# Fetching the turned rows on GpSimd's queue, and emitting row statistics and adjacency sums further behind their loads

## The chip, the cores and the metric

The kernel runs on one core of a Trainium2 chip. The core has five engines, each with an instruction queue that it works off in order: PE (TensorE, matrix products), DVE (VectorE), ACT (ScalarE), POOL (GpSimd) and SP (SyncE, which in this kernel only starts DMA transfers). An engine waits at an instruction until the semaphores of everything that it depends on have come. The metric is the device time of one execution in microseconds; lower is better.

## The reference

Two graph layers work on `x` of shape 128 x 128 x 256 (graphs, nodes, features) with an adjacency `adj` of 128 x 128 x 128. Cut to what matters:

```python
h = relu(layernorm(x))                       # layer 0
conv = relu(conv17(relu(conv1(h))) + h)      # along the nodes, with folded norms
msg  = relu(h @ w_msg + b_msg)
nmp  = (exp(-dist(h)) * adj) @ msg
x = x + gru(concat(conv, nmp), h)            # three gates

h = relu(layernorm(x))                       # layer 1, nodes 0..24 alone
for g, idx in enumerate(GROUPS):             # five groups of 25, 9, 7, 6, 6 nodes
    A = normalised(adj[:, idx][:, :, idx] + I)
    out = relu(A @ relu(A @ h[:, idx] @ W1[g] + b1[g]) @ W2[g] + b2[g])
    fused[:, idx] += softmax(fusion_w)[g] * out
x = x + fused
```

Layer 1 changes only the first 25 nodes of a graph. The other rows of the result are those of layer 0.

## The kernel before

Graphs are worked in 32 groups of four (`q`). The first 650 us or so do the convolution in frequency space, in two halves of 16 groups, and the messages of the groups that are ready. Then the last stage runs everything else together: `stage_c(q)` computes the gates of one group (matrix products of line 742; where no layer-1 work comes between, one group follows the next by some 33 us), and layer 1 follows in eight blocks of four groups.

The order in which instructions are emitted is set by a planner written into the kernel. Each piece of work is a generator, and each `yield cost, wait` says how much PE time the step just emitted is worth, and after how many further units of planned time its next step may be emitted. Lanes of generators are served by weight. The planner runs when the kernel is built; on the chip every engine simply takes its instructions in that order. A larger wait at a `yield` thus places the following instructions further back in their engines' queues; it makes nobody wait by itself.

The path of one group's result, with the lines that the change and the steps of the prediction touch:

- `stage_c` ends with the last gate sums on DVE (L854 to L867). PE's last product of the group goes into a bank that DVE must have read first (L862). POOL then runs six operations (L872 to L874, "the gates"), DVE turns the result (L897, emitted in the next group's `stage_c`) and adds the input rows (L904).
- `returned` stores the turned rows `xt` to DRAM (`x1d`) with four DMAs on POOL's queue (L906). The next group's input rows are loaded into the same buffer `xt` by POOL (L822).
- `fetch(q)` (L911 to L924) waits in the plan until `returned` has been emitted, then issues on SP's queue: L921 loads the first 32 nodes of the four graphs, 128 KB, into `X1`; L922 copies the other nodes, 384 KB, from `x1d` to the output, DRAM to DRAM. Both depend on the four stores.
- `rows(q)` (L963 to L980) computes mean and variance of the fetched rows on DVE (L971 to L973), the power -1/2 on POOL (L974), and the normalised rows `x1h` on DVE and ACT (L977, L978). They feed PE's L1058.
- `prepare(blk)` (L982 to L1044) loads the 25 x 25 adjacency of 16 graphs on SP (L990), adds the identity on POOL (L996, eight operations), sums rows on DVE (L1001), and makes the normalised adjacency with small PE products (L1007, L1012, L1033, L1038) and DVE and POOL operations between them; L1042 copies it to where L1058 reads it.
- `block(blk)` runs layer 1 for the block: L1058, then for each of the five groups two products (L1075, L1084). The weights `w1` are loaded on SP (L961) into two buffers, each load behind the last use of its buffer. At the end L1106, L1118 and L1128 turn, gather and fuse, and L1133 stores the rows on POOL's queue.
- SP's queue also holds the loads of `hTc` (L682), `xm` (L684) and `yt` (L606) for the next group.

Of the kernel before, what the change touches and what calls it, by code (L numbers as in the profile page):

```python
# [20 lines left out]
GB = 4  # L21
NQ = B // GB
# [9 lines left out]
QS = SB // GB  # L32
# [9 lines left out]
WIDE = 32  # L42


def _runs():

    out = []
    for g, nodes in enumerate(GROUPS):
        i = 0
        while i < len(nodes):  # L50
            j = i
            while j + 1 < len(nodes) and nodes[j + 1] == nodes[j] + 1:
                j += 1
            out.append((OFFS[g] + i, nodes[i], j - i + 1))
            i = j + 1
    return out
# [151 lines left out]
def kernel(ctx: ExitStack, tc: tile.TileContext, x, adj, consts, vecs, w_se, conv1_w,  # L208
                    conv2_w, w_msg, b_msg, w_ih, w_hh, W1, W2, b2, fusion_w, out):
    nc = tc.nc  # L210
# [15 lines left out]
    x1d = [dr.tile([GB, N, D], FP, name=f"x1d{q}") for q in range(NQ)]  # L226
# [7 lines left out]
    def c(name):  # L234
        a, b = CAT[name]
        return cst[:, a:b]
# [333 lines left out]
    EN, IN, IN2, X1, E_DONE, F_DONE = {}, {}, {}, {}, set(), set()  # L570
# [340 lines left out]
    def fetch(q):  # L911

        while q not in T_DONE:
            yield 0.0, 0.5
        yield 0.0, 12.0 if q < NQ - 1 else 6.0
        blk = q // QS
        while blk > 2 and blk - 3 not in F_DONE:
            yield 0.0, 0.5
        if blk not in X1:
            X1[blk] = LATE["co"].tile([P, QS, D], FP, tag="x1", name=f"x1_{blk}", bufs=3)  # L920
        nc.sync.dma_start(out=X1[blk][:, q % QS], in_=x1d[q][:, :WIDE])  # L921
        nc.sync.dma_start(out=out[q * GB:(q + 1) * GB, WIDE:], in_=x1d[q][:, WIDE:])  # L922
        yield 0.0, 5.0
        C_DONE.add(q)  # L924


# [55 lines left out]
    def prepare(blk):  # L982

        while not (blk - 1 in P_DONE and blk - 2 in {-2, *B1_DONE}):
            yield 0.0, 1.0
        pool, pool2, b1 = S["pool"], S["pool2"], S["b1"]
        ac, r4 = S["ac"][blk % 2], S["r4"][blk % 2]
        aj = pool.tile([NN, SB, NN], FP, tag="dd", name=f"aj{blk}")
        for i in range(GB):
            nc.sync.dma_start(out=aj[:, i % 2 * 2 + i // 2::GB],  # L990
                              in_=adj[blk * SB + i:(blk + 1) * SB:GB, :NN, :NN]
                              .rearrange("b n m -> n b m"))
        yield 0.0, 4.0

        for r, n, w in _runs():
            nc.gpsimd.tensor_tensor(b1[:, :, r:r + w], aj[:, :, n:n + w],  # L996
                                    ident[:NN, None, n:n + w].to_broadcast([NN, SB, w]),
                                    ALU.add)
        dg = pool2.tile([NN, SB, NG], FP, tag="dg", name=f"dg{blk}")
        for g in range(NG):  # L1000
            nc.vector.reduce_sum(dg[:, :, g], b1[:, :, OFFS[g]:OFFS[g] + SIZES[g]],  # L1001
                                 axis=mybir.AxisListType.X)
        yield 0.0, 7.0

        pa = ptmp.tile([P, SB // 2, RP], FP, tag="tmp", name=f"pa{blk}")
        for p in range(SB // 2):
            nc.tensor.matmul(pa[:, p], b1[:, 2 * p:2 * p + 2, :].rearrange("n s r -> n (s r)"),  # L1007
                             c("et")[:NN, :RP], start=True, stop=True)
        nc.vector.tensor_mul(ac, pa, c("same")[:, None, :].to_broadcast([P, SB // 2, RP]))

        pdg = ptmp.tile([P, SB // 2, 2, NG], FP, tag="tmp", name=f"pdg{blk}")
        nc.tensor.matmul(pdg.rearrange("p a s g -> p (a s g)"), c("et")[:NN],  # L1012
                         dg.rearrange("n b g -> n (b g)"), start=True, stop=True)
        dsel = pool.tile([P, SB // 2, 2 * NG], FP, tag="dsel", name=f"dsel{blk}")
        nc.vector.tensor_mul(dsel, pdg.rearrange("p a s g -> p a (s g)"),
                             c("sgrp")[:, None, :].to_broadcast([P, SB // 2, 2 * NG]))
        dm = pool.tile([P, SB // 2], FP, tag="dm", name=f"dm{blk}")
        zo = pool.tile([P, SB // 2], FP, tag="zo", name=f"zo{blk}")
        nc.vector.reduce_sum(dm, dsel, axis=mybir.AxisListType.X)
        nc.vector.tensor_scalar(zo, dm, 0.0, None, op0=ALU.is_equal)  # L1020
        nc.vector.tensor_add(dm, zo, dm)
        nc.gpsimd.tensor_tensor(dm, dm, c("mhalf"), ALU.pow)
        nc.gpsimd.tensor_mul(zo, zo, dm)
        nc.gpsimd.tensor_sub(dm, dm, zo)
        yield 2.0, 7.0

        dd = pool.tile([P, SB // 2, RP], FP, tag="dd", name=f"dd{blk}")
        nc.vector.tensor_mul(dd, c("diag")[:, None, :].to_broadcast([P, SB // 2, RP]),
                             dm[:, :, None].to_broadcast([P, SB // 2, RP]))
        nc.vector.tensor_mul(ac, ac, dm[:, :, None].to_broadcast([P, SB // 2, RP]))  # L1030
        yield 0.0, 6.0
        pg = ptmp.tile([P, SB // 2, RP], FP, tag="tmp", name=f"pg{blk}")
        nc.tensor.matmul(pg, c("ones2"), dd, start=True, stop=True)  # L1033
        nc.vector.tensor_mul(ac, ac, pg)
        yield 0.9, 3.0

        pr4 = ptmp.tile([P, QS, 2, RP], FP, tag="tmp", name=f"pr4{blk}")
        nc.tensor.matmul(pr4.rearrange("p q a r -> p (q a) r"), c("e4"), ac,  # L1038
                         start=True, stop=True)
        for j in range(GB):  # L1040
            s = slice(j * WIDE, (j + 1) * WIDE)
            nc.vector.tensor_copy(r4[s, :, j % 2 * 2 + j // 2, :], pr4[s, :, j % 2, :NR])  # L1042
        yield 0.9, 1.0
        P_DONE.add(blk)  # L1044
# [112 lines left out]
    for bat, (during_a, during_b) in enumerate(((0.66, 0.5), (0.2, 0.65))):  # L1157
        if bat:
# [12 lines left out]
    loads = Lane([stage_n(q) for q in range(NQ)])  # L1171
    groups = Lane([stage_c(q) for q in range(NQ)], ahead=2)
    second = [setup_1()] + [part(blk) for blk in range(NBLK) for part in (prepare, block)]
    beside.weight = 0.5
    order.run(loads, groups, beside, Lane([fetch(q) for q in range(NQ)], ahead=2),
              Lane([rows(q) for q in range(NQ)], ahead=2),
              Lane(second, ahead=2, weight=0.2))
# [41 lines left out]
```

## Time and profile before

| | us |
|---|---|
| median of three runs | 2040.95 |
| lowest and highest | 2039.93, 2042.65 |
| the profiled execution, its own time | 2045.82 |
| span of that execution, first to last instruction | 2043.9 |
| PE busy in it | 1975.7 |
| POOL busy in it | 865.4 |

The profile shows one execution. For every group of instructions it has the busy time and what ended the engine's idle time before it; a chain of waits follows the instruction that ended last back to what released it; busy time can be had for any stretch of the span, and every wait by the instruction that ended it. Names such as `x1d<-xt` say which tile is written and which is read.

### The profile page before, as it was taken

The page shows a single profiled execution, that of the slowest core. Times are in us where ns is not written, and L with a number is a line of the kernel's source. Part 1 is how long each engine was busy: PE and PEld are TensorE (multiplying, and loading weights), DVE is VectorE, ACT ScalarE, POOL GpSimd, SP SyncE. Part 2 cuts the span into 40 slices and gives each one's busy share as a digit, 9 for nine tenths or more (in the row PEclk, how much of TensorE's full clock was granted, in tenths as well). Part 3 has the DMA queues.
Part 4 walks back from the last instruction along what each step waited for, and adds up shares of the span by engine and source line. Part 5 has one row for each costly group of instructions (what it writes and reads, how often), then busy time and mean ns, then how long its engine had stood idle before and what let it go on. Part 6 is the DMA issues. An engine that isn't in the chain of part 4 may idle for free.

```text
span 2043.9 us, 33427 instructions
## 1 busy us (share of the span) xinstructions
PE 1975.7 (97%) x12596; PEld 1635.6 (80%) x12596; DVE 1327.4 (65%) x2807; ACT 683.3 (33%) x1547; POOL 865.4 (42%) x1026
## 2 busy tenths in 40 slices
PE   7998999999999999999889999999999999999988
PEld 5667888888888888878678878888788788888865
DVE  6774445875433667856774786778677868786542
ACT  4653222444222344222223232232323332322233
POOL 3542666333665133633441445335434444353330
PEclk9999999999999999999989999999999999999989
DMA  9987879654777644624423353343443533442331
GB/s 215 293 276 224 275 252 288 203 166 155 268 257 247 179 117 117 166 73 109 107 75 96 94 117 90 105 121 94 118 109 87 116 110 95 114 102 77 81 85 53
DMA packets 182583, 302.84 MB, mean 148 GB/s; under 512 B 24001, under 2 KB 131462, under 8 KB 182166
## 3 DMA queue, kind: packets, MB, share of 16 engines
q1 hardware_dynamic: 143238, 185.46, 31.6%
q0 software_dynamic: 38800, 114.96, 20.4%
q8 instruction: 100, 1.64, 0.3%
q14 instruction: 61, 0.50, 0.1%
q10 hardware_dynamic: 384, 0.28, 0.0%
HBM read 204.12 MB, written 109.05 MB: 153 GB/s over the span
## 4 chain that ended last, share of the span: by engine, by line
PE 83%; DVE 5%; DMA 5%; POOL 3%; issue 2%; SPq 1%; ACT 1%; DVEq 0%; POOLq 0%; ACTq 0%
PE p L742 38%; PE pa L527 7%; PE ph L1075 5%; PE pm L631 5%; PE pz L1084 5%; PE pc L422 4%; PE pb L527 3%; PE pf L433 3%; PE pi L699 3%; PE px L657 3%; PE pw L475 1%; PE ph L411 1%; PE py L1058 1%; DMA x1d<-xt 1%; DMA w<-in_W 1%
## 5 line engine op out<-in xcount | busy, mean ns | idle before, releaser
L906 POOL DMA_DIRECT2D x1d<-xt x128 | 101.3, 818 | 189.0 <-DVE xt L904 183.7
L822 POOL DMA_DIRECT2D xt<-in_x x128 | 100.5, 793 | 132.0 <-DMA x1d<-xt 130.1
L527 PE MATMUL pa<-wf,X 128*128 128x256 f32 x640 | 152.2, 381 | 0.0
L559 DVE SCALAR_TENSOR_TENSOR y<-pa,kk 128x512 f32<-128x512 f32 x78 | 53.8, 690 | 151.3 <-ACT kk L558 150.8
L872 POOL TENSOR_TENSOR hTc<-hTc,r 128x512 f32<-128x512 f32 x64 | 87.6, 1369 | 135.9 <-ACT r L869 135.9
L742 PE MATMUL p<-th,wrz 128*128 128x256 f32 x512 | 137.3, 391 | 0.0
L742 PE MATMUL p<-tm,wrz 128*128 128x256 f32 x512 | 133.8, 384 | 0.0
L742 PE MATMUL p<-tc,wrz 128*128 128x256 f32 x512 | 131.7, 380 | 0.0
L527 PEld LDWEIGHTS pa<-wf,X 128*128 128x128 f32 x640 | 118.1, 190 | 16.2 <-issue 2.0
L1075 PE MATMUL ph<-yz,w 128*128 128x96 f32 (+3 forms) x640 | 114.1, 335 | 10.8 <-DMA w<-in_W 9.8
L422 PE MATMUL pc<-c1w,hTa 128*128 128x256 f32 x512 | 121.1, 382 | 2.7 <-DVE X L439 1.5
L631 PE MATMUL pm<-wmsg,hT 128*128 128x256 f32 x512 | 122.7, 385 | 1.0 <-DVE xnmp L659 1.0
L897 DVE STREAM_TRANSPOSE hTc<-z 128x512 f32<-128x512 f32 x64 | 66.8, 1045 | 83.4 <-POOL z L874 83.4
L1075 PEld LDWEIGHTS ph<-yz,w 128*128 128x128 f32 x640 | 92.3, 202 | 31.9 <-issue 26.6
L1077 ACT ACTIVATE hh<-ph,vec 128x96 f32<-128x96 f32 (+3 forms) x160 | 63.6, 402 | 150.2 <-PE ph L1075 142.6
L711 ACT ACTIVATE xc<-xc,t_bn 128x256 f32<-128x256 f32 x128 | 58.1, 500 | 159.9 <-DVE xc L708 159.9
L742 PEld LDWEIGHTS p<-th,wrz 128*128 128x128 f32 x512 | 95.5, 192 | 18.8 <-issue 5.4
L742 PEld LDWEIGHTS p<-tm,wrz 128*128 128x128 f32 x512 | 99.0, 193 | 14.0
L631 PEld LDWEIGHTS pm<-wmsg,hT 128*128 128x128 f32 x512 | 96.5, 191 | 17.0 <-issue 1.6
L422 PEld LDWEIGHTS pc<-c1w,hTa 128*128 128x128 f32 x512 | 93.9, 190 | 19.9 <-DVE h L425 4.8
L742 PEld LDWEIGHTS p<-tc,wrz 128*128 128x128 f32 x512 | 97.6, 191 | 13.3
L1084 PE MATMUL pz<-hh,w 128*128 128x96 f32 (+3 forms) x640 | 107.7, 322 | 0.0
(198 smaller groups left out, 4688.9 us busy)
## 6 DMA issues: line engine op xcount, KB each, us to landing
wf<-wfd SPq DMA_DIRECT2D x160, 256.0 KB
wfd<-ws POOLq DMA_DIRECT2D x64, 320.0 KB, 9.6
yd<-y POOLq DMA_DIRECT2D x80, 256.0 KB, 4.3
yt<-yd SPq DMA_DIRECT2D x64, 320.0 KB
w<-in_W SPq DMA_DIRECT2D x40, 512.0 KB
xa<-in_x SPq DMA_DIRECT2D x128, 128.0 KB
hTd<-hTa POOLq DMA_DIRECT2D x32, 512.0 KB, 6.7
hT<-hTd SPq DMA_DIRECT2D x32, 512.0 KB
```

Source lines behind the costliest of these rows:

```text
L422: nc.tensor.matmul(pc[:, i], hT[:, k, (2 * h + i) * N:(2 * h + i + 1) * N], c1w[:, k], start=(k == 0), stop=(k == 1))
L433: nc.tensor.matmul(pf[:, i, :F * NB], h1[:, 2 * h + i, k * P:(k + 1) * P], fwd, start=True, stop=True)
L527: nc.tensor.matmul(ps, xk(k), WF[f][:, k, s], start=(k == 0), stop=(k == 1))
L631: nc.tensor.matmul(pm[:, i], hT[:, k, j * N:(j + 1) * N], LATE["wmsg"][:, k], start=(k == 0), stop=(k == 1))
L742: nc.tensor.matmul(ps[:, m], w[:, i, k, m * P:(m + 1) * P], factor(i, x, t), start=first and j == 0, stop=last and j == len(n) - 1, skip_g ...
L822: nc.gpsimd.dma_start(out=xt[a * WIDE:(a + 1) * WIDE].rearrange("p b d c -> p (b d) c"), in_=slices(x[q * GB:(q + 1) * GB])[a])
L872: nc.gpsimd.tensor_sub(d, d, r[:, dc])
L897: nc.vector.transpose(blocks(hT)[:, :, dc], z[:, dc].rearrange("p (s b) -> p b s", b=16))
L906: nc.gpsimd.dma_start(out=slices(x1d[q])[a], in_=xt[a * WIDE:(a + 1) * WIDE].rearrange("p b d c -> p (b d) c"))
L1075: nc.tensor.matmul(ph, w1[:, k, m * P:(m + 1) * P], yz[:, k, :, o:o + n], start=(k == 0), stop=(k == 1))
L1077: nc.scalar.activation(hh[:, m], ph, AF.Relu, bias=v("b1", g * 4 + m))
L1084: nc.tensor.matmul(pz, w2[:, g, m, cc * P:(cc + 1) * P], hs[g][:, m], start=(m == 0), stop=(m == 3))
```

## The change

Three edits in two functions. The row load and the copy of the other nodes go from SP's queue to POOL's. Their planned place behind the store is 5 units instead of 12 (6 for the last group), and the row statistics follow 9 units behind the fetch (4 for the last group) instead of 5. In `prepare`, the sums of the adjacency are emitted 13 units behind its load instead of 4. What is computed is the same.

```diff
         while q not in T_DONE:
             yield 0.0, 0.5
-        yield 0.0, 12.0 if q < NQ - 1 else 6.0
+        yield 0.0, 5.0
         blk = q // QS
         while blk > 2 and blk - 3 not in F_DONE:
             yield 0.0, 0.5
         if blk not in X1:
             X1[blk] = LATE["co"].tile([P, QS, D], FP, tag="x1", name=f"x1_{blk}", bufs=3)
-        nc.sync.dma_start(out=X1[blk][:, q % QS], in_=x1d[q][:, :WIDE])
-        nc.sync.dma_start(out=out[q * GB:(q + 1) * GB, WIDE:], in_=x1d[q][:, WIDE:])
-        yield 0.0, 5.0
+        nc.gpsimd.dma_start(out=X1[blk][:, q % QS], in_=x1d[q][:, :WIDE])
+        nc.gpsimd.dma_start(out=out[q * GB:(q + 1) * GB, WIDE:], in_=x1d[q][:, WIDE:])
+        yield 0.0, 9.0 if q < NQ - 1 else 4.0
         C_DONE.add(q)
...
                               .rearrange("b n m -> n b m"))
-        yield 0.0, 4.0
+        yield 0.0, 13.0
 
         for r, n, w in _runs():
```

## The prediction

> **What bounds the kernel now.** I read the page first, then busy time by stretch, then what PE waited for, then the chain around those waits, and last one undisturbed round of the loop.
>
> ```profile
> span 2043.9 us, 33427 instructions
> PE 1975.7 (97%) x12596; PEld 1635.6 (80%) x12596; DVE 1327.4 (65%) x2807; ACT 683.3 (33%) x1547; POOL 865.4 (42%) x1026
> ...
> PEclk9999999999999999999989999999999999999989
> ```
>
> PE is busy 97% of the span. Faster work elsewhere can only remove PE's idle time, and time at a lower clock. The two 8s in the clock row say where to look.
>
> ```profile
> 1000.00:1100.00 100.00, 86.15 (x473) 69.32 (x472) 64.18 (x125) 23.98 (x52) 37.36 (x45) 0.90 0.32 85
> 1100.00:1880.00 780.00, 779.40 (x4981) 649.86 (x4980) 572.92 (x1141) 229.26 (x502) 339.94 (x371) 1.00 0.41 105
> 1880.00:2044.00 164.00, 144.78 (x924) 113.75 (x922) 76.36 (x174) 49.40 (x111) 43.59 (x54) 0.95 0.29 72
> ```
>
> The columns are the stretch, its length, busy PE, weight loads, DVE, ACT, POOL, then clock, DMA share and GB/s. From 1100 to 1880 PE lacks 0.6 us: there is nothing to win there, only to lose. The gain lies near 1000 and after 1880.
>
> ```profile
> PE p L742 <- DVE r L862: 11.8, 7, 7.6
> PE ph L1075 <- DMA w<-in_W: 9.8, 2, 6.2
> PE py L1058 <- ACT x1h L978: 4.9, 2, 3.3
> PE py L1058 <- DVE r L1042: 2.5, 1, 2.5
> SPq L921 <- DMA x1d<-xt: 269.4, 58, 27.6
> ```
>
> These are waits (total, times, longest). The last line is SP's own queue: SP stands 269.4 us at the fetch, waiting for the turned rows to land in DRAM. Whatever is queued behind it waits too. Two places in the chain of waits show who pays (start, us, what):
>
> ```profile
> 1000.49 5.05 DMA x1d<-xt
> ...
> 1005.67 0.54 SPq L921
> ...
> 1008.44 10.39 DMA aj<-in_adj
> ...
> 1019.00 2.94 POOL b L996 x8
> ...
> 1022.13 0.41 DVE r L862
> ...
> 1022.59 2.09 PE p L742 x4
> ```
>
> ```profile
> 1960.35 5.97 DMA x1d<-xt
> ...
> 1966.34 0.54 SPq L921
> ...
> 1967.66 7.75 DMA w<-in_W
> ...
> 1975.55 3.72 PE ph L1075 x16
> ```
>
> In the first, the adjacency load waits behind the fetch; POOL's sums wait for it; DVE's row sums (L1001) stand in DVE's queue ahead of L862, which PE needs: PE idles 7.61 us. In the second, the W1 load waits behind the fetch and PE idles 6.24 us; the same happens at 1903.78 for 3.52 us.
>
> **What the Trainium skill says.** "DMA: Bandwidth & Descriptors", section "Anatomy of one DMA — SWDGE (gpsimd) path": a semaphore wait happens on the issuing sequencer before dispatch. The 269.4 us at L921 agree, so the change moves that wait from SP's queue to POOL's. The same page, "Issuing engines are not separate DMA queues": DMAs of all issuers interleave on the same 16 engines, so the transfer itself should not get quicker; no run here shows this yet. "TensorE: Matmul & The Clock Gate", "What's actually happening": after an idle window of about 3.4 us the array's clock is halved. The trace agrees: after the 7.61 us wait a pair of L742 matmuls takes 1.22 us against 0.59. "SBUF — State Buffer", "Who interferes with whom": a DVE operation in a two-port mode blocks GpSimd, and so its descriptors. Here it is not visible: 128 issues of L906 last 778 to 854 ns.
>
> **What can be removed.** From 880 to 1080 PE idles 2.53 (L1042), 7.61, 1.65, 1.33, 3.27 us and, near 877, 0.39 and 0.59: 17.4. The slow matmuls after it, start to start against the same groups at full clock, add 2.4 after 1022.6, 3.4 after 1032, 1.6 after 1074.6 and 1.0 after 890.8: 8.4. In the tail 3.52 + 6.24 = 9.8 idle and 1.8 + 2.1 slow: 13.7. Together 39.5 us, the most that the change can bring.
>
> **Part 1, the fetch moves to POOL.** 64 issues leave SP and come to POOL. SP's W1, adjacency, yt and hTc loads no longer stand behind x1d. Each round (32 of them) POOL gets two issues. The nearest rows are POOL's 128 KB stores L1133 (716 ns) and L822 (793 ns); I take 0.8 each. The DRAM-to-DRAM copy is not in POOL's trace; its issue could lie between SP's 0.63 and, bounded by POOL's longest issue, 0.86. That is 51 us on an engine 42% busy. The wait on x1d costs POOL little new: its next instruction, L822, already waits there (130.1 us in 30 waits) because xt is one buffer. Building the changed kernel shows its order in nearly every round: L906 four times, L921, L922, L822 four times, then L974. So L822, L974 and, in blocks, L996 come 1.6 us later.
>
> **When the rows arrive.** This round is undisturbed:
>
> ```profile
> 1361.05 3.18 POOL L906 DMA_DIRECT2D x1d<-xt  x4 [5.28 <-DVE xt L904]
> 1368.32 3.14 POOL L822 DMA_DIRECT2D xt<-in_x  x4 [4.09 <-DMA x1d<-xt]
> ...
> 1374.98 0.41 DVE L854 TENSOR_TENSOR r<-r,p 128x256 f32<-128x256 f32 x1
> ...
> 1377.80 0.42 DVE L971 BATCH_NORM_STATS2 st<-x 128x6 f32<-128x256 f32 x1
> ```
>
> Call 1361.05 T0. x1d lands at T0+7.0 and POOL reacts by T0+7.3. From SP the row load took 4.89 and 4.39 us from issue to its user in the two rounds where DVE waited for it. From POOL nothing shows it: x1d stores have a median of 4.8, L1133 5.3, and xt, also 128 KB but in 128-byte pieces, 8.7. Lower bound 4.4, upper 8.7; I take 4.9. The rows are there at T0+12.2.
>
> **Part 2, the statistics.** In most rounds the new order puts L971 to L973 just before L854, reached at about T0+13.0 to 13.9, formerly often after L862 (here T0+16.8). So at 4.9 us DVE does not wait, with about 1 us to spare, but the 0.75 us of the three operations now stands ahead of L862, for which PE waits directly. L862's slack is 0.9 to 1.6 us in most rounds without block work, so 0.65 remains. Two things eat it: hTc's 512 KB load now starts with x1d instead of after the fetch, and the round at 1091.70, where a W1 load did, had x1d landing at T0+8.96; and in two rounds four L1042 copies (1.5 us) come ahead of L862. I charge 3 us for all rounds, between 0 and 30 (rival below). L977 now stands before L867 and the slow tc subtractions, so the waits for x1h (4.9 us) go.
>
> **Part 3, the adjacency sums.** The load is no longer held up and the sums are emitted 9 units later, so the 7.61 us go. What is late next, from the order built, block by block.
>
> Block 0 (round at 859.61): L1001 stands before L824, L831 and L835, and L996 behind L921 and L922. L996 can run from T0+8.9 to T0+11.8, then DVE needs 3.4 us to L835 (1366.53 to 1370.35 elsewhere, less a 0.42 idle). PE wants L835's bank at T0+9.4: idle 6, with a late landing 7.7. I take 7.0 plus 2.5 of slow clock, as after the 7.61: 9.5.
>
> Block 2: L996 and L1001 stand directly behind the gates (L872 to L874), ahead of L793. In the round shown the gates ended at 1355.8 and L793 ran at 1356.8; with 2.95 us of L996 and a last sum of 0.25 it would run at 1359.2, 2.4 late. PE's next need in that row, L816 before the third wrz product, has 0.6 of slack and 2.2 us of pa and pdg in front of it, against 1.5 us of new DVE work: about 1 idle there, 1 at L862, 1 of clock: 3.
>
> Blocks 3 to 6: rounds with block work have 2.9 to 6 us of slack at L862: nothing. Were the cover gone, 3 us each.
>
> Block 7: L996 stands behind the last rows' L974. With T0 at 1958.06, x1d at T0+8.3, 4.9 for the rows, 0.75 of statistics, 0.56 of power and 3.0 of L996 pa (L1007) can run at 1975.9; PE, with no wait on W1, is there at about 1974.4: 1.6 idle. The four L1042 (1.5) and one L1130 (0.4) now stand between L1038 and L1058: 1.8 idle. 0.4 at W1 and 1.8 of clock: 5.6 in all.
>
> Rounds before 859: L675 stores wait 1.6 us longer: 1.5 in all.
>
> **Sum.** 39.5 removed, 9.5 + 3 + 3 + 5.6 + 1.5 = 22.6 new: 16.9 us less, a span near 2027. The profiled execution took 2045.8, of which 1.9 lie outside the span; the median shown, 2040.95, is 4.9 below it. The difference applied to the median: 2024.
>
> **Rivals.** *Nearly all of it goes* (13%): the aj load of block 0 is early and L996 finds POOL free, so 39.5 less about 8: 2009. For it: only the block-0 wait is large. Against: the in-order queue puts L996 behind the fetch.
>
> *Given back* (12%): small waits of 0.5 to 1 us at L862 in the 15 rounds with little slack take the 17 back: about 2039. For it: seven waits of 0.49 to 7.61 us on L862 already.
>
> *Slower* (25%): the row load from POOL takes as long as xt's, 8.7 us. The rows come at T0+16; DVE stands 2.7 us at L971, before L862, of which 0.65 is slack: 2.05 x 15 = 31 us, against the 20 of the sum without its 3 us: 11 slower, 2052. It decides from a landing of 8.0 us on (4.9 + 1.75 spare + 20/15). For it: no POOL load of such rows is in the trace, and an earlier hTc load delays x1d too. Against: L1133, of the same shape the other way, lands in 5.3.
>
> The forecast itself has 50%, with 2016 to 2032 as its own range.
>
> **The numbers.** Faster by over 0.2% (4 us, about what a measurement of this kernel can tell from no change): 50 + 13 + 5 of the give-back case. Same 7, slower 25. The range 2006 to 2052 leaves out about 2 in 10.
>
> **What would show it.** No SP wait at L921 and about 210 us or more of POOL waiting for x1d, now before L921; no PE wait on W1; no L1001 wait ahead of L862 in the round after block 1; a PE wait of 6 to 8 us near 870; DVE waits at L971 under 10 us in all. A stretch 1100 to 1880 with PE idle over 15 us, or L971 waiting for x over 1.5 us per round, would make the prediction wrong.

## The result and the profile after

| | before | after |
|---|---|---|
| median of nine runs, us | 2044.02 | 2035.45 |
| lowest and highest, us | 2037.36, 2050.84 | 2028.12, 2039.76 |
| ratio of after to before | | 0.9953, 95% interval 0.9931 to 0.9974 |
| span of the profiled execution, us | 2043.9 | 2038.0 |
| POOL busy in it, us | 865.4 | 906.6 |

The change makes the kernel faster by 0.47%, some 9.6 us with an interval from 5 to 14. (The ratio is that of the means; the two medians alone would give 0.9958.) The prediction, 2024 against 2040.95, was a ratio of 0.9917: the sign was right, the size was about 1.8 times what was measured.

The page of the changed kernel first, then busy time by stretch (columns as in the prediction):

```profile
PE 1977.1 (97%) x12596; PEld 1638.2 (80%) x12596; DVE 1313.6 (64%) x2807; ACT 682.5 (33%) x1547; POOL 906.6 (44%) x1090
...
PEclk9989999999999999989999999999999999999989
```

```profile
1000.00:1100.00 100.00, 98.43 (x607) 79.95 (x606) 71.15 (x148) 27.12 (x61) 50.06 (x61) 0.98 0.41 101
1100.00:1880.00 780.00, 775.95 (x4960) 647.57 (x4959) 559.76 (x1131) 227.95 (x499) 363.63 (x406) 0.99 0.40 104
1880.00:2038.00 158.00, 142.41 (x913) 112.67 (x911) 74.32 (x173) 48.54 (x109) 47.38 (x60) 0.96 0.29 71
```

Around 1000 the hole is filled: 98.43 us of PE in place of 86.15. From 1100 to 1880 PE now lacks 4.05 us where it lacked 0.6. After 1880 it still lacks 15.6 us, against 19.2: the tail gained much less than the W1 waits that left it. What PE and the two engines around the fetch waited for (total, times, longest):

```profile
PE p L742 <- DVE ve L835: 6.5, 1, 6.5
PE pa L1007 <- POOL b L996: 4.3, 1, 4.3
...
PE p L742 <- DVE r L862: 3.9, 8, 0.7
PE pzt L1106 <- DVE yz L1086: 2.8, 4, 1.5
...
DVE st L971 <- DMA x<-x1d: 17.9, 9, 6.5
...
POOL x L921 <- DMA x1d<-xt: 166.3, 30, 7.5
```

No line for W1 and none for SP at L921 is left. The largest waits of PE in the last stage are now two that were not there, both ending with POOL's eight L996. The end of the chain of waits shows the second (start, us, what):

```profile
1950.79 0.78 POOL x1d L906
...
1953.19 7.56 DMA x1d<-xt
...
1961.41 0.70 POOL x L921
...
1962.69 4.80 issue
...
1968.07 2.92 POOL b L996 x8
...
1971.04 3.67 PE pa L1007 x16
```

The stores of the last group land 10.0 us after the first of them, the last rows follow (in the 4.80 us called "issue", POOL stands at L974 until the rows and their statistics are there), and the adjacency sums of block 7 stand behind both. Then PE starts L1007, at about half speed: the same group takes 1.99 us elsewhere.

Two profiles can be compared step by step by the start of L904, which DVE runs once in each of the 32 rounds. Up to the first one (739.55 us before, 745.75 after) both kernels have the same instructions, so those 6.2 us are scatter between executions. From there on, the difference to the kernel before in us, for all kernels of this study. The end is the start of the last store to the output. Round n is the time from the nth L904 to the next; further on, a kernel is often called by the first part of its name (e1, b0):

| kernel | L904 1 to 10 | 10 to 30 | 30 to 31 | 31 to the end | sum | ratio in time (95% interval) |
|---|---|---|---|---|---|---|
| the change | -14.2 | +5.8 | -5.4 | +1.5 | -12.4 | 0.9953 (0.9931 to 0.9974) |
| e1_fetch_alone | -9.7 | +3.7 | -5.4 | +2.2 | -9.2 | 0.9947 (0.9930 to 0.9963) |
| e2_sums_alone | -20.9 | +0.9 | -0.5 | +3.0 | -17.6 | 0.9950 (0.9931 to 0.9969) |
| e3_fetch_on_SP | -23.0 | +3.1 | -0.7 | +3.3 | -17.4 | 0.9936 (0.9913 to 0.9959) |
| q1_queue_alone | -3.3 | +7.5 | -5.4 | +2.0 | +0.8 | 0.9990 (0.9973 to 1.0006) |
| b0_sums_before_store | -22.1 | +4.7 | -5.4 | +2.6 | -20.3 | 0.9901 (0.9881 to 0.9921) |
| b7_sums_before_fetch | -14.3 | +4.7 | -5.4 | -4.5 | -19.5 | 0.9923 (0.9903 to 0.9943) |
| b0b7_both | -24.7 | +5.1 | -5.4 | -6.3 | -31.4 | 0.9864 (0.9840 to 0.9888) |
| e7_copy_on_SP | -10.0 | +27.6 | 0.0 | +6.8 | +24.4 | 1.0149 (1.0116 to 1.0182) |
| m3_more_load_beside_stores | -12.2 | +5.5 | -5.4 | +1.7 | -10.4 | 0.9997 (0.9986 to 1.0008) |
| hyb_last_three_on_POOL | -22.9 | +0.3 | -5.4 | -4.8 | -32.9 | 0.9842 (0.9815 to 0.9869) |

The sums come from one execution each, the ratios from four to twenty. They agree within some 5 us for most, but in time e2 and m3 gain 7 and 10 us less than their profiles show, and e7 loses 6 more. Where the two differ, the sum tells in which stretch something happened in that execution, and the ratio how much the change of the kernel is worth.

### The profile page after: what moved, and what is told of

The parts are those of the page before. It is cut to its first block, busy times and chain, and to the rows that moved or that the text cites. A ratio compares the mean times of both kernels' runs of the same rounds, so it can differ in the third digit from the quotient of the medians.

```text
span 2038.0 us, 33376 instructions
## 1 busy us (share of the span) xinstructions
PE 1977.1 (97%) x12596; PEld 1638.2 (80%) x12596; DVE 1313.6 (64%) x2807; ACT 682.5 (33%) x1547; POOL 906.6 (44%) x1090
## 3 DMA queue, kind: packets, MB, share of 16 engines
q0 software_dynamic: 44944, 131.79, 22.9%
## 4 chain that ended last, share of the span: by engine, by line
PE 85%; DVE 6%; DMA 4%; POOL 2%; issue 2%; ACT 1%; SPq 0%; DVEq 0%; POOLq 0%; ACTq 0%
PE p L742 39%; PE pa L527 7%; PE pm L631 5%; PE ph L1075 5%; PE pc L422 4%; PE pz L1084 4%; PE pb L527 3%; PE px L657 3%; PE pf L433 3%; PE pi L699 2%; DMA x1d<-xt 1%; PE ph L411 1%; PE pw L475 1%; PE py L1058 1%; PE pa L1007 1%
## 5 line engine op out<-in xcount | busy, mean ns | idle before, releaser
L906 POOL DMA_DIRECT2D x1d<-xt x128 | 100.7, 811 | 167.4 <-DVE xt L904 156.0
L1075 PE MATMUL ph<-yz,w 128*128 128x96 f32 (+3 forms) x640 | 112.4, 331 | 1.0 <-issue 0.5
L1084 PE MATMUL pz<-hh,w 128*128 128x96 f32 (+3 forms) x640 | 109.6, 327 | 0.0
L1075 PEld LDWEIGHTS ph<-yz,w 128*128 128x128 f32 x640 | 91.3, 199 | 21.8 <-issue 15.5
L822 POOL DMA_DIRECT2D xt<-in_x x128 | 101.3, 798 | 4.7 <-DMA x1d<-xt 3.4
```

The source lines that it names most:

```text
L822: nc.gpsimd.dma_start(out=xt[a * WIDE:(a + 1) * WIDE].rearrange("p b d c -> p (b d) c"), in_=slices(x[q * GB:(q + 1) * GB])[a])
L906: nc.gpsimd.dma_start(out=slices(x1d[q])[a], in_=xt[a * WIDE:(a + 1) * WIDE].rearrange("p b d c -> p (b d) c"))
L1075: nc.tensor.matmul(ph, w1[:, k, m * P:(m + 1) * P], yz[:, k, :, o:o + n], start=(k == 0), stop=(k == 1))
L1084: nc.tensor.matmul(pz, w2[:, g, m, cc * P:(cc + 1) * P], hs[g][:, m], start=(m == 0), stop=(m == 3))
```

## The experiments

The theory after the result: the gain is short because block 0's and block 7's sums stand behind the fetch on POOL, and because SP, no longer held at the fetch, starts other transfers against the stores. The main rivals: that POOL's 64 extra issues cost something in every round, and that all of the gain comes from the sums. Blocks count from 0. The expectation of e1_fetch_alone speaks of block 1 where it means the sums that made the wait of 7.61 us near 1022; these are block 2's.

**The fetch without the sums (e1_fetch_alone).**

```diff
-        yield 0.0, 13.0
+        yield 0.0, 4.0
```

> The fetch on POOL's queue with its new places, but the adjacency sums back at 4 units behind their load. Theory (two separate gains): the tail gain belongs to the fetch, so PE's waits on W1 (9.8 us before) stay away; the L862 wait behind block 1's sums comes back smaller than 7.61 us, 2 to 4 us, because the load no longer stands behind the fetch; block 0's wait on L835 (6.5 us) is under 3. Ratio to before 0.992 to 0.997. Rival (all of the gain comes from the sums): no gain is left, ratio 0.999 or more.

Measured: no wait on W1; the L862 wait is 3.31 us in place of 7.61; L835 is gone from the list. But PE now waits 6.8 us at L1007 in the tail and 2.12 on L1042. The ratio is as expected, and so the gain of the change does not all come from the sums.

**The sums without the fetch (e2_sums_alone).** The kernel before with one line changed:

```diff
-        yield 0.0, 4.0
+        yield 0.0, 13.0
```

> The kernel before with the adjacency sums 13 units behind their load and nothing else. Theory (the fetch on POOL's queue costs in blocks 0 and in the middle about what it brings in the tail): block 0's L996 stands behind the store alone, so L835 waits under 2 us, the 7.61 us before L862 are gone, and the waits on W1 stay, 9 to 12 us; ratio to before 0.989 to 0.993, no worse than the whole change. Rival (the parts need each other): 0.996 or more.

The waits are as expected (L835 1.39 us, the 7.61 gone, W1 10.9), and the profile gains 17.6 us. The time, 0.9950, is just above the expected 0.989 to 0.993 and below the rival's 0.996. This one line is worth as much as the whole change.

**The queue alone (q1_queue_alone).** The kernel before with `nc.gpsimd` for `nc.sync` in L921 and L922, in their old places:

```diff
-        nc.sync.dma_start(out=X1[blk][:, q % QS], in_=x1d[q][:, :WIDE])
-        nc.sync.dma_start(out=out[q * GB:(q + 1) * GB, WIDE:], in_=x1d[q][:, WIDE:])
+        nc.gpsimd.dma_start(out=X1[blk][:, q % QS], in_=x1d[q][:, :WIDE])
+        nc.gpsimd.dma_start(out=out[q * GB:(q + 1) * GB, WIDE:], in_=x1d[q][:, WIDE:])
```

> The kernel before with L921 and L922 issued by POOL in their old places, behind the loads L822, and nothing else changed. Theory (the queue's own gain is W1 in the tail and an earlier adjacency load, its price later stores and, in blocks, sums behind the fetch): no PE wait on W1, the 7.61 us before L862 shrink to 2 to 4, rows come some 3 us later than in the changed kernel but their statistics stand later too; ratio to before 0.992 to 0.997. Rival (rows behind L822 come too late for L971 or x1h): waits at L971 or at L1058 for x1h of 15 us or more, ratio 1.000 or more.

The waits on W1 go, as expected, but the ratio is 0.9990: no gain that can be measured. PE waits 6.0 us at L1007, 3.9 on L1042 and up to 3.3 at L1106, and DVE 18.8 us at L971, as the rival said. Freeing SP's queue by itself buys nothing. e1 has the same queue and the old sums, and differs in the places of the fetch and of the statistics alone: its ratio is 0.9947. In the mean of the rounds, x1d lands 8.4 us after the first store in both, but POOL issues the row load after 9.0 us in e1 and, behind the four loads L822, after some 12 us in q1. So the new places of the fetch and the statistics carry a part of the gain.

**The new places with the fetch on SP (e3_fetch_on_SP).** The changed kernel with `nc.sync` in L921 and L922:

```diff
-        nc.gpsimd.dma_start(out=X1[blk][:, q % QS], in_=x1d[q][:, :WIDE])
-        nc.gpsimd.dma_start(out=out[q * GB:(q + 1) * GB, WIDE:], in_=x1d[q][:, WIDE:])
+        nc.sync.dma_start(out=X1[blk][:, q % QS], in_=x1d[q][:, :WIDE])
+        nc.sync.dma_start(out=out[q * GB:(q + 1) * GB, WIDE:], in_=x1d[q][:, WIDE:])
```

> The order of PE, DVE and ACT as in the changed kernel, but L921 and L922 issued by SP again. Theory (the queue matters: SP standing at the fetch is what delays W1): PE waits 8 us or more on W1 again, ratio to before 1.000 to 1.005. Rival (POOL's 64 extra issues eat the gain in every round): the waits on W1 are small, the stretch 1100 to 1880 is 3 to 6 us shorter than in the changed kernel, ratio 0.990 to 0.994.

Its list of waits has the W1 wait again, at full size:

```profile
PE ph L1075 <- DMA w<-in_W: 12.3, 3, 8.4
```

The theory was right in this, and wrong in the ratio: 0.9936, not 1.000 or more; this lies in the range of the rival. Its interval overlaps with that of the change, so neither queue is shown to be the faster one with these places. What the theory had left out is seen in the table. With the fetch off POOL, block 0's sums stand behind the store alone, and L835 waits 1.4 us in place of 6.5: 7.9 us in round 4. The middle is 2.7 us shorter too, of which 1.7 are a slow group in round 24 that comes by chance (see the end). By the profiles, with these places and sums, the move to POOL's queue brings 4.7 us between L904 30 and 31 and 1.8 after it, and costs 8.8 and 2.7 in the two stretches before.

**Block 0's sums ahead of the store (b0_sums_before_store).** The changed kernel, with the wait split so that L996 and L1001 can be placed apart; of all queues only POOL's order differs. In b7_sums_before_fetch the entry is `{7: (1.0, 7.0, 12.0)}`, and DVE's L1001 moves too.

```diff
-        yield 0.0, 13.0
+        w1, w2, w3 = {0: (2.0, 8.0, 7.0)}.get(blk, (13.0, None, 7.0))
+        yield 0.0, w1
...
                                     ALU.add)
+        if w2:
+            yield 0.0, w2
         dg = pool2.tile([NN, SB, NG], FP, tag="dg", name=f"dg{blk}")
...
-        yield 0.0, 7.0
+        yield 0.0, w3
```

> As the changed kernel, but block 0's eight L996 stand on POOL ahead of the store L906 instead of behind the fetch; the other engines' order is the same. Theory (L996 behind the fetch sets L835): PE's wait of 6.52 us on L835 near 881 falls under 1 us and the slow matmuls after it go, 7 to 9 us less, ratio to before 0.990 to 0.992. Rival (something else holds DVE there, or the later store gives it back): under 3 us less, ratio 0.994 to 0.996.

The wait, in this kernel's list:

```profile
PE p L742 <- DVE ve L835: 1.3, 1, 1.3
```

6.5 us became 1.3, a little more than expected, most of the slow matmuls behind it went, and round 4 is 8.5 us shorter than with the change; 7.9 of them are left at the end. Ratio 0.9901, as the theory said.

**Block 7's sums ahead of the fetch (b7_sums_before_fetch).**

> As the changed kernel, but block 7's L996 stand on POOL behind L906 and ahead of the fetch, and its L1001 on DVE ahead of L971; PE's order is the same. Theory (the tail's 4.28 us wait at L1007 comes from L996 standing behind the last rows' statistics): the wait falls under 0.5 us and the end comes 4 to 6 us sooner, ratio to before 0.992 to 0.994. Rival (the last rows' landing sets the end anyway): L1007's wait is replaced by one at L1058 of 3 us or more, ratio 0.995 to 0.996.

PE no longer waits at L1007, which takes 1.99 us instead of 3.67; the wait at L1058 stays at 1.1 us, so the last rows do not set the end. From L904 31 to the end the kernel is 5.9 us shorter. Ratio 0.9923.

**Both (b0b7_both).**

> As the changed kernel with both moves of the sums, block 0's ahead of the store and block 7's ahead of the fetch. Theory (the two waits are independent): the gains add, 8.5 and 5.9 us against the changed kernel; ratio to before 0.986 to 0.990. Rival (the tail's end or a slow clock takes one back): 0.990 or more.

0.9864, with L1007 gone from the list and 1.3 us left at L835: the two gains add.

**What makes x1d land late (e7_copy_on_SP).** In the mean of 32 rounds it takes 7.3 us from the first L906 to the first instruction that waits for x1d (L921 or L822) before, 8.6 with the change, 7.2 in e3. One round, in the timeline, first of the changed kernel, then of e3:

```profile
1130.18 3.15 POOL L906 DMA_DIRECT2D x1d<-xt  x4 [5.63 <-DVE th L587]
...
1130.51 0.46 SPq L961 DMA_DIRECT2D w<-in_W  x1
...
1131.07 0.42 SPq L682 DMA_DIRECT2D hTc<-hTd  x1
...
1139.97 0.72 POOL L921 DMA_DIRECT2D x<-x1d  x1 [6.63 <-DMA x1d<-xt]
...
1144.22 0.43 DVE L971 BATCH_NORM_STATS2 st<-x 128x6 f32<-128x256 f32 x1 [1.88 <-DMA x<-x1d]
```

```profile
1119.74 3.16 POOL L906 DMA_DIRECT2D x1d<-xt  x4 [5.29 <-DVE xt L904]
...
1127.44 0.54 SPq L921 DMA_DIRECT2D x<-x1d  x1
...
1128.70 0.44 SPq L961 DMA_DIRECT2D w<-in_W  x1
...
1129.26 0.40 SPq L682 DMA_DIRECT2D hTc<-hTd  x1
...
1132.52 0.43 DVE L971 BATCH_NORM_STATS2 st<-x 128x6 f32<-128x256 f32 x1 [0.27 <-DMA x<-x1d]
```

In the first, 1 MB of loads starts with the stores, and the row load is issued 9.8 us after the first store; in the second SP stands until x1d is there, issues the row load after 7.7 us, and starts the other loads behind it. DVE's 1.88 us at L971 reach PE as 1.51 us at L1106 in this round. To tell this from a slower reaction of POOL, the copy alone went back to SP, so that SP stands again:

```diff
-        nc.gpsimd.dma_start(out=out[q * GB:(q + 1) * GB, WIDE:], in_=x1d[q][:, WIDE:])
+        nc.sync.dma_start(out=out[q * GB:(q + 1) * GB, WIDE:], in_=x1d[q][:, WIDE:])
```

> As the changed kernel, but the copy of the other nodes (L922) is issued by SP, in the same place, so that SP stands for x1d again while the row load (L921) stays on POOL. From the first store to L921 it takes 8.6 us in the mean in the changed kernel and 7.2 with the fetch on SP. Theory (SP, no longer standing, starts hTc, W1 and yt loads against the stores): the mean falls to 7.0 to 7.6, the wait of 1.51 us at L1106 near 1147 goes, and PE waits 8 us or more on W1 again. Rival (POOL reacts later to the landing than SP does): the mean stays at 8.3 or more. Ratio to before: 0.993 to 0.998 by the theory, as the middle gains 2 to 4 us and the tail loses 5.

The mean falls from 8.6 to 7.66, just above the 7.6 of the theory and most of the way to 7.2, with POOL still the one that reacts. What is left is POOL's reaction. The traces also tell when the last of the four stores landed, in the mean so long after the first was issued, and how long after that the row load was issued, in the median:

| kernel | last store landed, us | row load issued after that, us |
|---|---|---|
| before | 7.2 | 0.1 (SP) |
| the change | 8.1 | 0.6 (POOL) |
| e3_fetch_on_SP | 7.1 | 0.1 (SP) |
| e7_copy_on_SP | 7.1 | 0.6 (POOL) |
| m3_more_load_beside_stores (below) | 8.8 | 0.6 (POOL) |

So both were right in part: of the 1.4 us between e3 and the change, some 1.0 is a later landing, and the rest is POOL's slower reaction, as the rival said. PE waits 14.3 us on W1 again, as expected.

The ratio, 1.0149, was expected by neither: it comes from the next transfer. In this kernel's lists of waits and of DMA issues (last number: median us to landing):

```profile
DVE st L971 <- DMA x<-x1d: 66.0, 24, 8.3
...
x<-x1d POOLq DMA_DIRECT2D x32, 128.0 KB, 8.0
```

And in the changed kernel's list of DMA issues:

```profile
x<-x1d POOLq DMA_DIRECT2D x32, 128.0 KB, 4.2
```

SP's copy of 384 KB and its held-back loads now start within about a microsecond of the row load, the copy ahead of it (in the round above at 1133.05 and 1133.54), and the row load takes 8.0 us instead of 4.2. The stretch between L904 10 and 30 is 21.8 us longer than with the change. In e3, where the same transfers follow the row load on one queue, the load of the round above took 5.1 us to its user.

**More load beside the stores (m3_more_load_beside_stores).**

```diff
         nc.sync.dma_start(out=hT, in_=hTd[q])
+        nc.sync.dma_start(out=dr.tile([P, 2, 512], FP, name=f"dup{q}"), in_=hTd[q])
```

> As the changed kernel, and SP issues one more transfer right behind each hTc load: hTd copied once more, 512 KB, to a DRAM tile that nobody reads, so that twice as much runs beside the stores of xt. The result stays the same. Theory (transfers that SP starts beside the stores make x1d land late): from the first store to L921 it takes more than the 8.6 us of the changed kernel, 9.5 or more in the mean, DVE waits 40 us or more at L971 instead of 17.9, and the ratio to before is 1.00 or more. Rival (8.6 instead of 7.2 is POOL's slower reaction to the landing): the mean stays at 8.3 to 8.9, the waits at L971 under 25 us, ratio 0.993 to 0.998.

The mean rises to 9.3 us, a little short of the expected 9.5. POOL's reaction stays at 0.6 us, so all of the rise is the landing, 8.8 us after 8.1. With e7 this settles the direction: less beside the stores, sooner; more, later. The gain of the change is gone in time: 0.9997. That the later landing took it is not shown: DVE's wait at L971 rises only to 23.2 us, PE now also waits 3.3 us on yt, and in the profile the sum from the first L904 on is only 2 us worse than that of the change, while the part ahead of it, with the same work for PE, took 5.8 us longer than before. Why the times show no gain stays open.

**A version from these findings (hyb_last_three_on_POOL).** The fetch on SP, where its stand shields the stores, except for the last three groups, where W1 loads stand behind it; and block 7 as in b7_sums_before_fetch.

```diff
+        eng = nc.gpsimd if q >= NQ - 3 else nc.sync
-        nc.gpsimd.dma_start(out=X1[blk][:, q % QS], in_=x1d[q][:, :WIDE])
-        nc.gpsimd.dma_start(out=out[q * GB:(q + 1) * GB, WIDE:], in_=x1d[q][:, WIDE:])
+        eng.dma_start(out=X1[blk][:, q % QS], in_=x1d[q][:, :WIDE])
+        eng.dma_start(out=out[q * GB:(q + 1) * GB, WIDE:], in_=x1d[q][:, WIDE:])
```

> The places of the changed kernel, the fetch on SP except for the last three groups, which POOL issues, and block 7's sums ahead of the fetch. Theory (SP's stand at the fetch costs only where a W1 load is behind it, in the tail, and shields the stores elsewhere): no wait on W1, block 0's wait under 2 us, the stretch between the tenth and the thirtieth L904 1.5 to 3 us shorter than in the changed kernel; from the first L904 to the end 28 to 32 us less than before, ratio 0.984 to 0.988. Rival (W1 waits come elsewhere): 0.990 or more.

2012.78 us in the median against 2043.75, a ratio of 0.9842: 1.6% under the kernel before. W1 waits are down to 1.2 us in all, the time from the first store to the fetch to 7.3, and the middle costs 0.3 us in place of 5.8, more than was expected. The interval overlaps with that of b0b7_both, so neither of the two is shown to be the best.

## Why the prediction was right in sign and too large in size

Its steps against the profile of the change, from the first L904 on:

| step of the prediction | predicted, us | measured, us |
|---|---|---|
| early rounds, L904 1 to 4 | +1.5 | -0.5 |
| near 880 to 1130, L904 4 to 10: 25.8 removed, 9.5 and 3 new | -13.3 | -13.7 |
| all rounds, L904 10 to 30 | +3 | +5.8 |
| first W1 wait, L904 30 to 31 | -5.3 | -5.4 |
| second W1 wait (8.3) less block 7 (5.6), to the end | -2.7 | +1.5 |
| sum | -16.8 | -12.4 |

**Block 0 was right.** The wait at L835 was forecast as 6 to 7.7 us and is 6.52; with the slow clock it was put at 9.5, and b0 takes back 8.5 with 1.3 us of wait left. That it was hidden in the sum as a cost, and not seen as something to avoid, is the lesson: b0 and b7 move one block's sums each and together bring more than the whole change.

**The step that failed is block 7, "5.6 in all".** Its place was right, L1007 behind L996 behind L974; its size was 9.8, which the trace gives term by term. PE idles 4.28 us at L1007, not 1.6, and 1.14 at L1058, not 1.8. The slow clock after it costs 1.68 on L1007, 0.26 on L1012, 1.7 on the next L1075 and 0.74 on L1084, 4.4 us against the 1.8 of the prediction. The idle time is longer mainly because "x1d at T0+8.3" was taken from the kernel before. It landed at T0+10.0, and POOL issued the row load at T0+10.6. SP, free now, had started two W1 loads of 512 KB at 1952.16 and 1954.12, beside the last stores; that such loads delay the landing is what e7 and m3 show. The prediction had moved the W1 loads forward and counted only what they no longer cost. The slow clock also lasts longer, as it does wherever L1007 comes early after a wait: in the ten places of these profiles where it follows within 2 us of the end of a wait of over 2.4 us, the clock is at half for 7.2 to 11.3 us after PE resumes. After the five waits of over 6 us in which L1007 does not follow, four of them at W1, it is 4.2 to 4.9 us.

**The same omission is in "all rounds", 3 us.** The prediction named the cause, hTc's load starting with x1d, and then kept the undisturbed landing of T0+7.0; the mean with the change is 8.1, and the row load is issued at 8.7, where the prediction had T0+7.3. Of the 5.8 us, 1.8 are the round shown above, which e3 does not lose. Another 1.85 are in round 21, which e1 does not lose and e3 does (and e2 loses 1.4 there), so they come with the later sums, in a part of the kernel where the prediction had charged nothing. A further 1.8, in round 24, are a slow group of the kind described at the end; with the same order on PE, b0 and b0b7 have it too, and e3, b7 and m3 do not, so this part is chance. The 1.5 us that were charged for the early rounds did not show in this profile and make up for some of what was missed.

**The row load on POOL's queue was right.** 4.9 us was taken, between 4.4 and 8.7; it is 4.2. The rival "slower" rested on 8.7 here, with a cost of 31 us in the middle; its turning point was a landing of 8.0, with a cost of 20. e7 happens to be near that case: 8.0 us, and 27.6 us in that stretch. The mechanism of the rival was sound, and its premise did not hold for the change.

The other tests of the prediction: no SP wait at L921, no PE wait on W1 and no wait of 7.61 us before L862, as said. POOL waits 166 us at L921, not 210 or more. DVE waits 17.9 us at L971, where under 10 was said, still below the 1.5 us per round that would have refuted it. POOL's 41 us of added busy time are seen to hurt in one place: in the chain that leads to the wait of 6.52 us at L835, the two issues L921 and L922 stand for 1.3 us between the landing and L996. Elsewhere these runs do not show that the issues themselves cost anything.

The remaining distance, from 12.4 us in the profile to 9.6 in the times, lies within the interval of the ratio. What the planner's new order changed in round 21, instruction by instruction, was not followed further.

## What to carry to other kernels

A queue that stands at a wait also holds back the transfers behind it. Before freeing it, list what it will start, when, and which transfer on the critical path is in flight at that moment. When a wait moves to another in-order queue, look for the few instructions behind it that lead to the busiest engine, and place these first; here two such places were worth more than the change. And a stand that does harm in one place only is best removed in that place only.

## What the runs showed of the hardware

Landing times depend on what starts beside a transfer, on whichever queue. The four stores had landed, in the mean, 7.1 us after the first was issued when SP stood (e3), 8.1 with SP's loads beside them and 8.8 with 512 KB more (m3). POOL issued what waited for them 0.6 us after that, SP 0.1. The row load of 128 KB took 4.2 us in the median on POOL's queue with the copy behind it on the same queue, and 8.0 when SP's copy and loads started beside it on another. The Trainium skill says in "DMA: Bandwidth & Descriptors", "Issuing engines are not separate DMA queues", that DMAs of all issuers interleave on the same engines; the later landings of e7 and m3 agree with it.

PE's clock also falls with no idle time before it. Behind block 5's L1007 (16 matmuls of 64 columns with 25 rows, where most of the others have 128) the same group of L1084, in the same order, took, in the timelines of the change and of e3:

```profile
1672.76 3.79 PE L1084 MATMUL pz<-hh,w 128*128 128x144 f32 x16
```

```profile
1661.69 2.12 PE L1084 MATMUL pz<-hh,w 128*128 128x144 f32 x16
```

The clock granted to PE is 0.5 of full speed for 3.4 us there, from 1672.9 on. Such stretches cost 1.5 to 1.7 us each and come in some profiles and not in others with the same order. From the first L904 on, the twelve profiles have 29 of them, each 3.4 us long, with no wait of PE over 0.15 us in the 7 us before. All 29 begin 0.2 to 1.3 us behind the end of one of the 96 groups of L1007 (L1012, with 25 rows too, stands between). "TensorE: Matmul & The Clock Gate", "What's actually happening", ties the slow clock to an idle window of about 3.4 us; here PE was never idle by the profile. That the sparse L1007 counts as idle would fit these 29 places, and also the longer slow time where L1007 comes first after a wait. No run changed L1007, so it was not tested.
